# Two layers of graph attention on one core: the second tile's count and the first tile's columns put ahead of two projections in the first part

## Chip, core and metric

The kernel runs on one core of one Trainium2 chip. The metric is the device time of one execution in microseconds (us). The engines work side by side, each through its own queue of instructions in order: PE (TensorE, matrix multiplication; its weight loads are shown apart as PEld), DVE (VectorE), ACT (ScalarE), POOL (GpSimd), and SP (SyncE), which here only issues transfers (DMAs). POOL issues transfers too.

## What is computed

Two layers of graph attention over 3327 nodes with 1024 features, one adjacency matrix for both, each followed by a residual and a layer norm. Cut to what matters:

```python
# layer 0: 8 heads of 128
h = (x @ W).reshape(C, H, D)
alpha_src, alpha_dst = (h * a_src).sum(-1), (h * a_dst).sum(-1)
e = leaky_relu(alpha_src[i] + alpha_dst[j], 0.2);  e = -inf where adj[i, j] == 0
x = layernorm(x + softmax(e) @ h)
# layer 1: one head over 1024 features
h = x @ W1
e = leaky_relu(h @ a1 + (h @ a2).T, 0.2);  e = -9e15 where adj == 0
x = layernorm(x + relu(softmax(e) @ h))
```

The adjacency is symmetric with ones on its diagonal and very sparse: about 0.24% of the pairs are drawn, and each draw counts both ways.

## The kernel before, in words

The nodes are split into 26 tiles of 128 rows (NT = 26). The kernel has a first part that every input goes through, a flag that it computes, and then one of two arms: a dense one, and a sparse one, which this input takes. The sparse arm fetches, for each target tile, the rows of its neighbours with indirect transfers (L803) from a table in memory, h0_d for layer 0 and y_d for layer 1, and adds them with small matmuls.

The first part does two things at once. It projects every tile (x @ W, extended by score columns) and writes the table h0_d; and it turns each tile's 128 rows of the mask into lists of neighbours. Its instructions are put into the queues by hand: the order of the calls in the code is the order on each engine.

The projection of a tile t:

- `load_x(t)`: SP loads the rows; `flip(t)`: 8 transposes on PE in two groups (L176), each followed by copies on ACT and, elsewhere, DVE (in the trace, L179 on ACT).
- `project(t, c)` for c = 0, 1, 2: one third of the columns each, 8 multiplications, which the trace shows as 16 matmul instructions (L479), into one of two PSUM banks with the tag "A".
- `keep(t, c)`: ACT copies the result to SBUF (L496). With c = 2 it also takes out the scores (sd, L491) and two exponentials (L493, L494), and calls `factors(t)`: one ACT operation (r, L295) and four small POOL ones (L296 to L299). After the third keep of a tile SP writes it to h0_d (L499).

The lists of a tile t, class `Edges`:

- `count(t)` calls `words(t)` and then `load_mask(t + 3)`. `words`: POOL clears the diagonal of the mask (`affine_select`, L308); ACT sums each row (junk, L311, with a read of the accumulator) and makes deg_b of it (L313); DVE folds the mask into words in three steps (wd, L318). `load_mask` is a transfer that POOL issues (L468) into one of four mask buffers in turn (the last tile has a fifth), so `load_mask(4)` refills the buffer of tile 0.
- `keys` (two halves) and `columns` (two halves): DVE alone, picking the largest values and removing them (L274, L276, L360, L369 to L375).
- `ends(t)`: one matmul with deg_b (L327), one ACT copy (cnt, L328), seven small POOL operations (L335 to L341). `ends2(t)`: the same manner, matmul L346, ACT L347, POOL L348 to L353.
- `places` (ACT away L384 and L385, DVE L388 to L392), `give` (the xp matmuls, L411 and L401), `take` (ACT L423 to L428), `sources` (DVE L436 to L450).

A generator, `listing()`, strings these steps together. For the first tile its first four steps are the two halves of keys and the two halves of columns; the next, `count(3)`, then the places of tile 0. In the steady loop over tiles 3 to 25, `project` calls `pace()` after every second multiplication, which takes as many steps as keep the lists level with the projections. The start is written out call by call, and there the change lies: projections with `False` don't call `pace()`.

Of the kernel before, what the change touches and what calls it, by code (L numbers as in the profile page):

```python
# [26 lines left out]
def kernel(  # L27
# [129 lines left out]
    class Phase:  # L157
# [7 lines left out]
        def bank(self, tag, shape, name, dt=F32):  # L165
            return self.psum.tile(shape, dt, tag=tag, name=name, bufs=self.banks[tag])
# [286 lines left out]
    with ExitStack() as own, tc.manual_schedule():  # L453
# [10 lines left out]
        def load_mask(t):  # L464
            if t < NT:
                ads[t] = masks[t % 4 if t < NT - 1 else 4]
                for r in pieces(t):
                    nc.gpsimd.dma_start(ads[t][r, :N], adj[at(t, r), :])  # L468
# [6 lines left out]
        def project(t, c, paced=True):  # L475

            acc = accs[t, c] = bank("A", [P, CUTS0[c + 1] - CUTS0[c]], "mm")
            for k in range(KT):
                nc.tensor.matmul(  # L479
                    acc, xT[t][:, k, :], wt[:, k, CUTS0[c] : CUTS0[c + 1]], start=k == 0, stop=k == KT - 1  # L480
                )
                if paced and k % 2 == 1:
                    pace()

        def keep(t, c):
            if t not in hts:
                hts[t] = ph.sbuf("ht", [P, HW0], 4)
            ht, acc, c0 = hts[t], accs.pop((t, c)), CUTS0[c]
            m = min(CUTS0[c + 1], D) - c0
            if c == 2:  # L490
                nc.scalar.activation(sd0[:, t].rearrange("p a h -> p (a h)"), acc[:, m:], AF.Copy)  # L491
                lists[t].factors()
                nc.scalar.activation(ht[:, D : D + H], acc[:, m + H :], AF.Exp)  # L493
                nc.scalar.activation(ht[:, D + H :], acc[:, m + H :], AF.Exp, scale=SLOPE)  # L494
                scored.add(t)
            nc.scalar.activation(ht[:, c0 : c0 + m], acc[:, :m], AF.Copy)  # L496
            kept[t] = kept.get(t, 0) + 1
            if kept[t] == 3:
                nc.sync.dma_start(h0_d[t * P : (t + 1) * P, :], hts.pop(t))  # L499

        def count(t):
            if t < NT:
                lists[t].words(ads.pop(t), junk)
                load_mask(t + 3)

        def listing():

            for t in range(-1, NT):
                old, new = lists[t] if t >= 0 else None, lists[t + 1] if t + 1 < NT else None
                for s in range(4):  # L510
                    if old:
                        old.give(s)
                    if new:
                        (new.keys, new.columns)[s // 2](s % 2)
                    if s == 1 and 2 < t + 3 < NT:
                        lists[t + 3].ends(tri_b)
                    if s == 3 and 2 < t + 3 < NT:
                        lists[t + 3].ends2(all_b)
                    yield
                if old:  # L520
                    old.give(EB)
                    old.take()
                count(t + 4)
                yield
                if old:
                    old.sources()
                    yield
                while new and t + 1 not in scored:
                    yield
                if new:  # L530
                    new.places()
                    yield

        scored, kept = set(), {}
        steps, slots, done = listing(), [0, 0], [0]

        def pace():

            slots[0] += 1
            while done[0] * slots[1] < slots[0] * (7 * (NT + 1)):  # L540
                done[0] += 1
                next(steps, None)
# [90 lines left out]
        count(0)  # L633
        for _ in range(2):
            next(steps)
        project(2, 1, False)
        keep(2, 1)
        project(0, 2, False)
        keep(0, 2)
        lists[0].ends(tri_b)  # L640
        count(1)
        for _ in range(2):
            next(steps)
        project(1, 2, False)
        keep(1, 2)
        lists[0].ends2(all_b)
# [585 lines left out]
```

## Time and profile before

| what | value |
|---|---|
| median of 3 runs | 1955.56 us (1948.99 to 1957.19) |
| the profiled execution | 1903.19 us, of which its span is 1901.5 us |
| mean granted TensorE clock in it | 0.905 |
| first part, from the start to the flag | about 480 us |
| layer 0, sparse arm | about 480 to 1200 us |
| layer 1, sparse arm | about 1200 to 1901 us |

The profile describes one execution, the profiled one, and its stages are told by its clock, from the start of the span. Busy time of each engine by stretch (length; PE, PEld, DVE, ACT and POOL busy with their numbers of instructions; granted TensorE clock; busy share of the 16 DMA engines; GB/s):

```
478.00:530.00 52.00, 17.93 (x301) 14.42 (x301) 22.02 (x54) 4.11 (x15) 31.68 (x30) 0.66 0.90 342
530.00:1200.00 670.00, 401.27 (x7803) 335.39 (x7803) 429.48 (x1038) 166.81 (x485) 437.45 (x416) 0.79 0.98 376
1200.00:1901.00 701.00, 653.41 (x3717) 278.79 (x3717) 295.08 (x856) 144.91 (x253) 440.28 (x441) 0.98 0.93 354
```

Layer 0 has its DMA engines busy nearly all the time, layer 1 has PE busy. In lists of waits and in the timeline, "<-" names what ended an idle time: the engine, what it wrote, and its line. "issue" is time in which an engine waited for nothing that the profile shows.

### The profile page before, as it was taken

Reading aid. Unit: us, or ns where it says so; the run is one execution under the profiler, and the core shown is the slowest. Engines: PE = TensorE matmul, PEld = TensorE weight load, DVE = VectorE, ACT = ScalarE, POOL = GpSimd, SP = SyncE. Lnnn points to the kernel's source line nnn. Section 1 sums busy time; section 2 is a strip of 40 time slices with the busy share of each in tenths; the row PEclk is TensorE's granted clock in tenths of the full one; section 3 lists DMA queues with packets and bytes.
Section 4 is the critical chain, followed back from the end, with each engine's and each line's share of the span. In section 5 each row is a group of like instructions: output and inputs, shape, how many; then the busy total and the mean of one; then the engine's idle time right before and its main releaser. Section 6 shows DMA issues by size and latency. Waiting matters only on the chain.

```text
span 1901.5 us, 38079 instructions
## 1 busy us (share of the span) xinstructions
PE 1518.5 (80%) x14663; PEld 902.4 (47%) x14663; DVE 1146.6 (60%) x3058; ACT 546.6 (29%) x1422; POOL 1030.2 (54%) x1391
## 2 busy tenths in 40 slices
PE   8799999999266555656556565399999999999997
PEld 5465556666255554545545454144444444444443
DVE  6699999986386665666666666244444444444442
ACT  5544455542022222222222222012222212222220
POOL 4322222220576666676676764677766667666650
PEclk9899999999678777787788877699999999999999
DMA  7656455411899999999999997899999999999980
GB/s 184 101 133 131 100 99 99 88 62 39 325 373 404 396 392 394 366 405 392 386 392 389 394 376 273 332 398 410 400 372 382 380 378 369 359 371 373 366 326 33
DMA packets 171068, 567.76 MB, mean 299 GB/s; under 512 B 27690, under 2 KB 34346, under 8 KB 170878
## 3 DMA queue, kind: packets, MB, share of 16 engines
q0 software_dynamic: 131056, 455.68, 67.6%
q1 hardware_dynamic: 39822, 109.56, 15.4%
q8 instruction: 118, 1.93, 0.4%
q14 instruction: 72, 0.59, 0.1%
HBM read 578.85 MB, written 42.97 MB: 327 GB/s over the span
## 4 chain that ended last, share of the span: by engine, by line
PE 52%; DMA 24%; DVE 12%; ACT 6%; issue 4%; POOL 2%; SPq 0%; DVEq 0%; ACTq 0%; POOLq 0%
DMA src<-h_d,idx 20%; PE mm L1025 20%; PE acc L993 12%; PE mm L479 12%; DVE e L870 3%; PE acc L898 3%; ACT junk L311 3%; PE tr L176 2%; POOL src L803 2%; DMA src<-y_d,idx 2%; DVE pr L931 1%; PE acc L882 1%; DMA wt<-in_L_gnn_W_dram 1%; ACT xT L179 1%; PE xp L411 1%
## 5 line engine op out<-in xcount | busy, mean ns | idle before, releaser
L803 POOL DMA_INDIRECT src<-h_d,idx x416 | 441.1, 1060 | 209.1 <-PE acc L898 58.0
L803 POOL DMA_INDIRECT src<-y_d,idx x416 | 415.7, 999 | 221.6 <-PE acc L993 96.3
L898 PE MATMUL acc<-src,e 128*32 128x128 f32 x6656 | 278.5, 337 | 253.6 <-DVE e L870 253.5
L479 PE MATMUL mm<-wt,xT 128*128 128x347 f32 (+1 forms) x1248 | 402.3, 469 | 3.3 <-DMA wt<-in_L_gnn_W_dram 2.9
L1025 PE MATMUL mm<-wt,xT 128*128 128x512 f32 x832 | 383.3, 604 | 0.8 <-DVE o L1028 0.8
L898 PEld LDWEIGHTS acc<-src,e 128*32 128x32 f32 x6656 | 234.8, 137 | 311.3 <-DVE e L870 284.3
L479 PEld LDWEIGHTS mm<-wt,xT 128*128 128x128 f32 x1248 | 228.3, 192 | 106.0 <-issue 4.2
L1025 PEld LDWEIGHTS mm<-wt,xT 128*128 128x128 f32 x832 | 152.2, 190 | 199.5 <-issue 179.1
L993 PE MATMUL acc<-src,es 128*32 128x342 f32 (+1 forms) x2496 | 206.2, 464 | 33.8 <-DVE es L984 31.0
L870 DVE TENSOR_TENSOR e<-oh,way 128x1024 f32<-128x1024 f32 x130 | 158.7, 1221 | 63.2 <-ACT w L868 62.8
L993 PEld LDWEIGHTS acc<-src,es 128*32 128x32 f32 x2496 | 71.6, 111 | 158.6 <-issue 112.9
L868 ACT ACTIVATE w<-way 128x32 f32<-128x32 f32 (+1 forms) x130 | 24.6, 189 | 407.7 <-DVE way L866 395.6
L1028 DVE SCALAR_TENSOR_TENSOR o<-mm,y 128x512 f32<-128x512 f32 x52 | 35.9, 691 | 166.2 <-PE mm L1025 166.2
L1007 ACT ACTIVATE z<-y,ri 128x342 f32<-128x342 f32 (+1 forms) x78 | 39.5, 570 | 313.9 <-DVE ri L1003 313.9
L865 DVE TENSOR_TENSOR way<-src,re 128x32 f32<-128x32 f32 x104 | 20.8, 200 | 175.1 <-DMA src<-h_d,idx 157.6
L179 ACT ACTIVATE xT<-tr 128x512 f32<-128x512 f32 x104 | 59.4, 596 | 151.0 <-PE tr L176 150.9
L981 DVE TENSOR_TENSOR way<-way,src 128x128 f32<-128x128 f32 x104 | 31.1, 299 | 90.0 <-ACT way L951 44.2
L850 ACT ACTIVATE own<-own,es 128x128 f32<-128x128 f32 x208 | 63.6, 388 | 57.4 <-DVE es L847 57.4
L311 ACT ACTIVATE junk<-ad 128x3328 uint8<-128x3328 uint8 x26 | 78.4, 3014 | 2.5 <-POOL ad L308 2.5
L882 PE MATMUL acc<-end,e 128*128 128x128 f32 x416 | 67.7, 328 | 13.3 <-DVE e L870 13.3
L296 POOL CAST mvs<-r 128x8 bf16<-128x8 f32 x26 | 6.0, 232 | 122.8 <-ACT r L295 122.8
L335 POOL TENSOR_TENSOR place_of<-cnt 128x1 f32<-128x1 f32 x26 | 4.9, 190 | 121.0 <-ACT cnt L328 101.5
(188 smaller groups left out, 1959.7 us busy)
## 6 DMA issues: line engine op xcount, KB each, us to landing
h_d<-ht SPq DMA_DIRECT2D x26, 520.0 KB
own<-h_d SPq DMA_DIRECT2D x26, 520.0 KB
y_d<-y SPq DMA_DIRECT2D x26, 514.0 KB
y<-y_d SPq DMA_DIRECT2D x26, 514.0 KB
x<-in_x_dram SPq DMA_DIRECT2D x25, 512.0 KB
y<-in_x_dram SPq DMA_DIRECT2D x25, 512.0 KB
out_dram<-o SPq DMA_DIRECT2D x25, 512.0 KB
ad<-in_adj_dram POOLq DMA_DIRECT2D x25, 415.9 KB
```

The source lines that it names most:

```text
L176: nc.tensor.transpose(tr[:, k, :], src[:, (4 * g + k) * P : (4 * g + k + 1) * P], ident)
L179: nc.scalar.activation(part, tr, AF.Copy)
L311: nc.scalar.activation(junk, ad, AF.Copy, accum_out=self.deg)
L479: nc.tensor.matmul(acc, xT[t][:, k, :], wt[:, k, CUTS0[c] : CUTS0[c + 1]], start=k == 0, stop=k == KT - 1)
L803: nc.gpsimd.indirect_dma_start(out=s[:, g, :w], out_offset=None, in_=table[:, :], in_offset=bass.IndirectOffsetOnAxis(ap=idx[:, t, b * NG ...
L850: nc.scalar.activation(hn, hn, AF.Copy, scale=es[:, n : n + 1])
L870: nc.vector.tensor_tensor(e, oh.unsqueeze(2).to_broadcast([P, ng, H, wide]), wp.unsqueeze(3).to_broadcast([P, ng, H, wide]), OP.mult,)
L882: nc.tensor.matmul(self.acc[h // 4][:, h % 4, :], e[:, 0, h, :], rowsof[:, 0, h, :], start=False, stop=h % 4 == 3,)
L898: nc.tensor.matmul(self.acc[h // 4][g * GT : (g + 1) * GT, h % 4, :], e[:, g, h, :], rowsof[:, g, h, :], start=first and h % 4 == 0, stop= ...
L993: nc.tensor.matmul(self.acc[c][to, :m], es[:, g, :], s[:, g, CUTS[c] : CUTS[c + 1]], start=b == 0, stop=b == EB,)
L1007: nc.scalar.activation(z[:, cut], self.res[:, cut], AF.Copy, scale=ri[:, 1:2])
L1025: nc.tensor.matmul(acc, xT[:, k, :], wt1[:, k, half], start=k == 0, stop=k == KT - 1)
```

## The change

Four lines move up by five calls. In the start of the first part, `count(1)` and the next two steps of the listing, which are the two halves of the columns of tile 0, now come straight after `count(0)` and the two halves of the keys, ahead of `project(2, 1)`, `keep(2, 1)`, `project(0, 2)`, `keep(0, 2)` and `lists[0].ends(tri_b)`. `count(1)` brings along its `load_mask(4)`. No instruction is added or removed.

```diff
         count(0)
         for _ in range(2):
             next(steps)
+        count(1)
+        for _ in range(2):
+            next(steps)
         project(2, 1, False)
         keep(2, 1)
         project(0, 2, False)
         keep(0, 2)
         lists[0].ends(tri_b)
-        count(1)
-        for _ in range(2):
-            next(steps)
         project(1, 2, False)
         keep(1, 2)
         lists[0].ends2(all_b)
```

What follows in the code is unchanged: `lists[1].ends(tri_b)`, `flip(3)`, `load_x(5)`, `flip(4)`, `count(2)`, and then the paced projections.

## Prediction

> **What bounds the kernel now.** I read the page first, for its stages, then the busy time in stretches of 4 us around the place of the edit, then the waits between 54 and 74 us, the timeline there, and last the chain of waits.
>
> ```profile
> span 1901.5 us, 38079 instructions
> PE 1518.5 (80%) x14663; PEld 902.4 (47%) x14663; DVE 1146.6 (60%) x3058; ACT 546.6 (29%) x1422; POOL 1030.2 (54%) x1391
> 0.00:478.00 478.00, 445.89 (x2842) 273.80 (x2842) 400.02 (x1112) 230.75 (x669) 120.79 (x505) 0.99 0.49 104
> ```
>
> The third line gives the first part (0 to 478 us): length, busy us of PE, PEld, DVE, ACT, POOL, granted clock, DMA share, GB/s. PE works 446 of 478 us, so what fills or makes a PE gap here counts. All moved instructions run between 45 and 65 us. The waits of 54 to 74 us show where PE stands still there (who waited, for whom, us in total, times, longest):
>
> ```profile
> PE xp L411 <- DVE place L391: 7.3, 1, 7.3
> PE op L327 <- ACT deg_b L313: 1.9, 1, 1.9
> PE tr L176 <- ACT cnt L328: 0.7, 1, 0.7
> DVE wd L318 <- POOL ad L308: 8.0, 2, 6.6
> ```
>
> The timeline gives their place (start, duration, engine, line, operation, idle before it and its releaser):
>
> ```profile
> 48.89 0.19 ACT L311 ACTIVATION_READ_ACCUMULATOR junk<-ad 128x1 f32 x1
> 49.12 0.21 ACT L313 ACTIVATE deg_b<-cnt 128x1 bf16<-128x1 f32 x1
> 50.34 0.46 ACT L496 ACTIVATE ht<-mm 128x347 f32<-128x347 f32 x1 [1.02 <-PE mm L479]
> ...
> 54.83 4.90 PE L479 MATMUL mm<-wt,xT 128*128 128x346 f32 x16
> ...
> 58.26 2.98 ACT L311 ACTIVATE junk<-ad 128x3328 uint8<-128x3328 uint8 x1 [2.31 <-POOL ad L308]
> ...
> 61.36 0.21 ACT L313 ACTIVATE deg_b<-cnt 128x1 bf16<-128x1 f32 x1
> 61.47 0.17 ACT L491 ACTIVATE sd<-mm 128x16 f32<-128x16 f32 x1
> 61.62 0.16 PE L327 MATMUL op<-deg_b,tri_b 128*128 128x1 bf16 x1 [1.89 <-ACT deg_b L313]
> 62.46 1.09 PE L176 MATMUL tr<-ident,x 128*128 128x128 f32 x8 [0.68 <-ACT cnt L328]
> ```
>
> The count of tile 1 (junk, 58.26) stands behind the seven small POOL operations of `ends(0)`, because its `affine_select` (L308, 57.94) does. It ends with deg_b at 61.57. PE had finished `project(1, 2)` at 54.83 + 4.90 = 59.73; the keep of that result (sd, L491) starts only at 61.47, behind the count on ACT, and PE's next instruction, the matmul of `ends(1)`, waits 1.89 us for deg_b. The chain runs here junk, deg_b, sd, r, the POOL operations of `factors(1)`, `ends2(0)`, `ends(1)`, the `affine_select` of tile 2, then
>
> ```profile
> 65.77 3.08 ACT junk L311 x2
> 68.87 0.04 ACT deg_b L313
> 68.91 0.06 issue
> 68.98 3.06 ACT junk L311 x2
> ```
>
> then the away operation, place (72.91) and PE's first xp matmul at 73.46, which ends the 7.3 us gap.
>
> **What the Trainium skill says.** "PSUM — Partial Sum Buffer", section "Engine vs sequencer instructions": the queues of ScalarE, VectorE and GpSimdE are strict FIFO. So an instruction put ahead delays all behind it if it waits. The trace agrees: sd (L491) has its data at 59.73 and starts when deg_b ahead of it is through, at 61.47. "TensorE: Matmul & The Clock Gate", section "What's actually happening": a pause of one window of about 3.4 us halves PE's clock, and the window runs freely. The trace agrees in kind: after the 7.3 us gap four matmul instructions took 2.67 us, against 1.33 us at 64.78. "DMA: Bandwidth & Descriptors", section "Issuing engines are not separate DMA queues": loads from SP and POOL share 16 engines. Here the engines have room where the moved load goes: their share is 0.00 in 52 to 56 us.
>
> **The change, part by part.** Nothing is added or removed. `count(1)` and columns(0) go ahead of two projections with their keeps and ahead of `ends(0)`.
>
> *PE and SP*: the order of their instructions is unchanged, since count, columns and key steps at this point issue none. SP's write of h0_d(0) and its loads pass nothing.
>
> *DVE*: its order is unchanged too; the projections and keeps moved past issue nothing there. It only stops waiting: the 6.60 us before wd at 58.26. Words of tile 1 (0.59 + 0.67) follow the keys at 51.66 and end near 52.9; columns(0) took 59.48 to 64.4, 4.9 us, and end near 57.9. This gain of 6.5 us has no taker, as its next work, the words of tile 2 (65.77), waits for POOL and its place step for ACT's away. Value 0.
>
> *POOL*: `affine_select` (0.29) and the issue of `load_mask(4)` (0.62) leave 57.94 to 58.79 and come after the issue of mask 3 (ends 45.65). The select needs mask 1, issued at 23.72; the DMA share is 0.81 in 28 to 32 us and 0.01 in 32 to 36, so it landed before 36. The select runs at 45.67. `load_mask(4)` refills the buffer of mask 0 and must wait for ACT's reading of it, through deg_b at 49.33 (the trace shows this very wait once, 2.5 us for deg_b, at the load issued at 69.13). Behind it on POOL is `factors(0)`, due at 55.49: 49.33 + 0.6 = 49.9, cover 5.6 us. Cost 0. The mask itself comes 8 to 9 us earlier, into free engines, and its first user, at 85.25, followed POOL's own work and not a landing. Value 0.
>
> *ACT*: junk(1) and deg_b(1), 58.26 to 61.57 = 3.31 us with the accumulator read, go ahead of keep(2, 1). New times: 49.33 to 52.6. Keep(2, 1) then runs 52.6 to 53.1 instead of 50.34 to 50.80, 2.3 us late. Its PSUM bank is next wanted by `project(1, 2)` at 54.83: cover 1.7 us. Keep(0, 2) starts with PE's end at 55.00, as now. Cost 0, with a thin cover.
>
> *What comes off the path*: deg_b(1) exists at 52.6, long before PE wants it, and ACT is free when `project(1, 2)` ends. sd then starts at 59.73 + 0.05 = 59.78 (the pair of 54.96 and 55.01 in the chain shows the 0.05) and not at 61.47: 1.69 us. The PE wait of 1.89 us goes; the next PE wait, for cnt (L347, 0.75 after sd, its keep lying between), shifts with sd: the flip starts near 60.75 instead of 62.46. POOL was in chain from r (61.67) to the select of tile 2 (65.75) without slack and shifts by the same 1.69; its own select and load no longer lie ahead of it. Then junk(2), junk(3), away, place, xp follow as before: xp at 71.77 instead of 73.46. What is late next is ACT's pair of counts, whose 7.3 us gap stays entire.
>
> *Whether it arrives at the end*: from 73.46 to 475 us I followed the chain: PE matmuls, ACT counts, DVE keys and lists alternate, and no DMA is in it, so there is nothing fixed in time to wait at, and no later order differs. At 480 us a flag is read, then the gathers start; they too shift. Forecast: -1.7 us in the profiled execution, 1901.5 to 1899.8.
>
> *Not shown by this trace*: the phase of the clock window after the 7.3 us gap. Slow matmuls cost (2.61 - 1.27) + (3.50 - 2.53) = 2.3 us by the chain. With the gap 1.7 us earlier the slow stretch can be shorter or longer; bounds, an estimate from these 2.3 us and the page's window: half a window, 1.7 us, either way. I take 0.
>
> The profiled execution took 1903.19 us, with 1.69 us around its span. The median of the runs shown is 1955.56, 52 us more, with the reason in no view; the gain lies in a stage at clock 0.99, so I carry it over as it is: 1955.56 - 1.7 = 1953.9.
>
> **The rivals.**
> *Absorbed, no gain*: 1955.6. For it: in 150 to 400 us DVE is on the chain again and again (92.8 busy of 100 in 300 to 400), and the second part is bound by gathers at a DMA share of 0.98. Against it: the order there is untouched and every queue is shifted alike.
> *The count blocks ACT, slower*: place, junk(1) ahead of keep(2, 1). If the select of tile 1 came no earlier than now (57.94), ACT would stand before keep(2, 1) until junk ends; deg_b at 61.57, keep to 62.0, and `project(1, 2)`, waiting for the bank, would run 62.0 to 66.9, its sd at 67.0 against 61.47: +5.5, so 1961. It decides from junk(1) starting after 49.33 + 1.7 (cover used up) + 1.7 (gain used up) = 52.7. Against it: mask 1 landed some 10 us before the select's new place, and POOL is free at 45.65.
> *More than forecast*: DVE's 6.5 us turn out useful, or the shorter low stretch of PE spares the slow clock after the gap. At most 1.7 + 2.3 + 1.7 = 5.7: 1950. Against: the gap of 7.3 us stays, and DVE waits for POOL anyway.
>
> **How the numbers follow.** Forecast 0.60, absorbed 0.24, blocked 0.09, more 0.07. The runs before spread from 1948.99 to 1957.19, so a median of a few runs can miss by about 4 us: this, more than any cost, makes the range. From 1950 - 4 = 1946 to 1961, opened by a little because the 52 us between profile and runs are unexplained: 1945 to 1962. About 0.5%, 9.8 us, is what a measurement of this kernel can tell from no change; no case reaches it without noise or an unseen effect: faster 0.06, same 0.85, slower 0.09.
>
> **What would show it.** Right: junk(1) starts at 49.3, the load of mask 4 is issued near 49.4, the wait of PE for deg_b is gone, the flip of tile 3 starts near 60.8, the first xp near 71.8, and the first part ends 1.7 us earlier. Wrong: a new PE wait for keep(2, 1) (L496) before 54.83, a POOL wait reaching past 55.5, junk(1) still behind `ends(0)`, or a first part that ends where it does now.

## The result and the profile after

The changed kernel takes 1958.89 us (median of 16 runs, 1950.73 to 1971.35), the kernel before, run beside it, 1958.56 us (16 runs, 1948.99 to 1968.26). The ratio is 1.0011, with a 95% interval of 0.999 to 1.0032: no difference that the measurement can tell. The forecast, 1.7 us less or 0.9991, lies inside the interval, and so does no change at all. The median lies in the stated range of 1945 to 1962 us and 5.0 us above the 1953.9 that was forecast; 3.0 us of these are the base, which was 1955.56 us as the median of three runs and is 1958.56 as that of sixteen, and the other 2.0 are within the scatter of the runs. A range that holds no change as well says little about the mechanism, so what the edit did has to be read from the trace.

The page of the changed kernel, its lines on the span and the engines, and the busy time of the first part (columns as before):

```profile
span 1958.3 us, 38079 instructions
PE 1661.6 (85%) x14663; PEld 936.8 (48%) x14663; DVE 1143.4 (58%) x3058; ACT 546.2 (28%) x1422; POOL 1028.7 (53%) x1391
```

```profile
0.00:478.00 478.00, 447.20 (x2842) 274.35 (x2842) 399.65 (x1111) 230.88 (x669) 121.49 (x505) 0.98 0.49 104
```

The span is 57 us longer than in the profile of before, with the same number of instructions, and the first part is not where it lies: the flag comes at 480.93 us, against 480.16. Before any cause is sought in the edit, the same kernels must be profiled again: the experiments begin with that.

The waits of the changed kernel between 54 and 74 us:

```profile
PE xp L411 <- DVE place L391: 7.3, 1, 7.3
DVE wd L318 <- POOL ad L308: 6.2, 1, 6.2
...
PE tr L176 <- ACT cnt L328: 1.0, 1, 1.0
```

PE's wait of 1.9 us for deg_b is gone, the gap of 7.3 us ahead of the first xp is entire. The timeline of the changed kernel, at the place of the edit:

```profile
50.62 0.21 ACT L313 ACTIVATE deg_b<-cnt 128x1 bf16<-128x1 f32 x1
50.73 2.96 ACT L311 ACTIVATE junk<-ad 128x3328 uint8<-128x3328 uint8 x1
50.89 0.55 POOL L468 DMA_DIRECT2D ad<-in_adj_dram  x1 [3.34 <-ACT deg_b L313]
...
53.82 0.20 ACT L313 ACTIVATE deg_b<-cnt 128x1 bf16<-128x1 f32 x1
53.93 0.44 ACT L496 ACTIVATE ht<-mm 128x347 f32<-128x347 f32 x1
...
56.33 4.90 PE L479 MATMUL mm<-wt,xT 128*128 128x346 f32 x16
...
61.10 0.16 PE L327 MATMUL op<-deg_b,tri_b 128*128 128x1 bf16 x1
61.27 0.18 ACT L491 ACTIVATE sd<-mm 128x16 f32<-128x16 f32 x1 [3.81 <-PE op L327]
...
62.28 1.09 PE L176 MATMUL tr<-ident,x 128*128 128x128 f32 x8 [1.02 <-ACT cnt L328]
```

This execution reached the place of the edit 1.5 us later than the profiled one of before (`project(1, 2)` at 56.33, not 54.83), so absolute times can't be compared. Counted from `project(1, 2)`, sd comes after 4.94 us, against 6.64 before: 1.70 us earlier. Marks used below: A, the start of tile 0's `affine_select` (L308); B, PE's matmul of `ends(0)` (L327), just ahead of that projection; X, PE's first xp matmul.

### The profile page after: what moved, and what is told of

Read it like the earlier page. It is cut to its first block, busy times and chain, and to the rows that moved or that the text cites. A ratio compares the mean times of both kernels' runs of the same rounds, so it can differ in the third digit from the quotient of the medians.

```text
span 1958.3 us, 38079 instructions
## 1 busy us (share of the span) xinstructions
PE 1661.6 (85%) x14663; PEld 936.8 (48%) x14663; DVE 1143.4 (58%) x3058; ACT 546.2 (28%) x1422; POOL 1028.7 (53%) x1391
## 4 chain that ended last, share of the span: by engine, by line
PE 72%; issue 11%; DVE 7%; ACT 5%; DMA 3%; POOL 1%; another core or an unknown queue 1%; SPq 0%; POOLq 0%; ACTq 0%; DVEq 0%
PE mm L1025 19%; PE acc L898 17%; PE acc L993 12%; PE mm L479 12%; PE acc L882 4%; PE acc L890 3%; ACT junk L311 2%; PE tr L176 2%; DMA src<-y_d,idx 1%; DMA wt<-in_L_gnn_W_dram 1%; PE den L907 1%; POOL src L803 1%; DMA src<-h_d,idx 1%; PE xp L411 1%; DVE top L274 1%
## 5 line engine op out<-in xcount | busy, mean ns | idle before, releaser
L898 PE MATMUL acc<-src,e 128*32 128x128 f32 x6656 | 379.3, 304 | 168.3 <-issue 135.3
L993 PE MATMUL acc<-src,es 128*32 128x342 f32 (+1 forms) x2496 | 215.2, 467 | 40.7 <-DVE es L984 24.7
L882 PE MATMUL acc<-end,e 128*128 128x128 f32 x416 | 94.3, 418 | 1.7 <-DVE e L870 1.7
L882 PEld LDWEIGHTS acc<-end,e 128*128 128x128 f32 x416 | 87.7, 321 | 2.3 <-DVE e L870 1.8
L1001 DVE TENSOR_TENSOR ri<-acc,es 128x1 f32<-128x1 f32 x26 | 4.1, 158 | 125.0 <-PE acc L993 110.2
```

The costliest lines, as they stand in the source:

```text
L882: nc.tensor.matmul(self.acc[h // 4][:, h % 4, :], e[:, 0, h, :], rowsof[:, 0, h, :], start=False, stop=h % 4 == 3,)
L898: nc.tensor.matmul(self.acc[h // 4][g * GT : (g + 1) * GT, h % 4, :], e[:, g, h, :], rowsof[:, g, h, :], start=first and h % 4 == 0, stop= ...
L993: nc.tensor.matmul(self.acc[c][to, :m], es[:, g, :], s[:, g, CUTS[c] : CUTS[c + 1]], start=b == 0, stop=b == EB,)
```

## The experiments

Each line is one profiled execution (of a timed kernel, the one of its runs that was profiled); all times in us.

| run | B to sd of tile 1 | B to X | PE's gap before X | B to the flag | span |
|---|---|---|---|---|---|
| before, first profile | 6.67 | 18.66 | 7.34 | 425.36 | 1901.5 |
| before, again | 6.68 | 19.19 | 6.42 | 426.64 | 1901.6 |
| columns alone ahead | 6.68 | 19.15 | 6.21 | 427.07 | 1899.9 |
| changed, first profile | 4.97 | 16.96 | 7.33 | 424.63 | 1958.3 |
| changed, again | 4.97 | 16.95 | 7.33 | 424.30 | 1894.9 |
| count alone ahead | 4.96 | 16.95 | 7.32 | 424.52 | 1895.2 |
| changed, timed | 4.96 | 16.97 | 7.34 | 424.48 | 1957.3 |
| count(2) early too | 4.97 | 13.78 | 4.14 | 420.85 | 1892.9 |
| count(2) ahead of keep(2, 1) | 6.28 | 15.08 | 4.14 | 422.93 | 1895.5 |
| changed, pacing lower | 4.97 | 16.96 | 3.85 | 423.51 | 1897.6 |
| count(2) early, pacing lower | 4.96 | 13.77 | 0.65 | 417.50 | 1892.0 |
| the same, timed | 4.96 | 13.79 | 0.67 | 417.54 | 1962.2 |

**Both kernels again.** No edit.

> The kernel before, unchanged, profiled once more. Two marks: A, the start of tile 0's affine_select (L308), and X, PE's first xp matmul (L411). Theory (the edit's own effect sits between A and X, the rest is scatter of one execution): X - A is 28.6 us again, as in the first profile of before, whatever A itself is, and the span comes out near 1957, not 1901.5, so the 57 us between the first two profiles are not the edit's. Rival (the changed order costs time later): the span is again near 1901.

> The changed kernel, unchanged, profiled once more. Theory: X - A is 26.9 us again, 1.7 less than before. From A to the flag (L699) it needs between 433.5 and 435 us: the first profiles show 435.32 before and 434.60 after, and the slow stretch of PE after the gap moves this by about 1 us either way. Rival (the 1.7 us were luck of one execution's start): X - A lies between 27.5 and 28.6.

Before: X - A was 29.14 where 28.6 was expected, and the span 1901.6 where I had expected 1957. Changed: X - A 26.92 as expected, A to the flag 434.27, span 1894.9. So the 57 us come and go with the same kernel: the changed one has spans of 1894.9 and 1957.3. Between these two, B to the flag is 424.30 and 424.48; the flag to the first gather of y_d takes 714.6 and 751.6, the rest 701.1 and 725.8. The two were run on different chips, and the longer one shows a wait that the other doesn't. PE's largest wait between 530 and 1190 us, first the changed kernel as timed (1957.3), then the changed kernel again (1894.9):

```profile
PE acc L898 <- issue: 137.4, 349, 1.1
```

```profile
PE acc L898 <- DVE e L870: 227.4, 95, 6.2
```

In the longer one PE halts 349 times for nothing that the profile shows. Whether the chip or something else makes it do so was not tried; it is no work of the edit, as the kernel before, timed beside the longer one, took as long (1953.22 to 1972.27 us).

The 0.5 us that the kernel before took longer to X the second time is PE's clock. PE from the matmul of `ends(1)` to the first quarter of `project(2, 2)`, in the second profile of before:

```profile
61.70 0.16 PE L327 MATMUL op<-deg_b,tri_b 128*128 128x1 bf16 x1 [1.89 <-ACT deg_b L313]
62.53 1.09 PE L176 MATMUL tr<-ident,x 128*128 128x128 f32 x8 [0.68 <-ACT cnt L328]
63.88 1.97 PE L176 MATMUL tr<-ident,x 128*128 128x128 f32 x8 [0.25 <-ACT xT L179]
65.64 1.99 PE L479 MATMUL mm<-wt,xT 128*128 128x346 f32 x4
```

The second group of eight transposes took 1.97 us and the four matmuls 1.99, against 1.15 and 1.33 in the first profile. The granted clock, third number from the end of the line for 64 to 66 us, was halved, first the first profile of before, then the second:

```profile
64.00:66.00 2.00, 2.00 (x12) 1.29 (x10) 0.64 (x2) 1.55 (x4) 1.77 (x10) 1.00 0.94 324
64.00:66.00 2.00, 2.00 (x9) 1.98 (x10) 0.60 (x3) 1.02 (x3) 1.77 (x10) 0.50 0.91 322
```

In the second it is 0.50 from 63.57 to 66.98 us, and PE was busy for 1.20 us of the 3.41 us ahead of that. The late copies then held ACT's count of tile 2 back by 0.5 us.

**The two halves of the edit apart.** The edit moves three lines, the count and the two-line loop of the columns. The count alone, shown against the changed kernel, and the columns alone, against the kernel before:

```diff
         count(1)
-        for _ in range(2):
-            next(steps)
...
         lists[0].ends(tri_b)
+        for _ in range(2):
+            next(steps)
```

> Only count(1) goes ahead, the columns of tile 0 stay where they were. Theory (ACT's and POOL's place for the count is the whole effect, DVE's place is worth nothing): X - A is 26.9 us as with the full change; DVE ends the columns about 4.9 us after ends(0), before its words of tile 2. Rival (the columns count too): X - A is over 27.3.

```diff
         count(0)
-        for _ in range(2):
+        for _ in range(4):
             next(steps)
...
         count(1)
-        for _ in range(2):
-            next(steps)
```

> Only the columns of tile 0 go ahead, count(1) stays behind ends(0). Theory: X - A is 28.6 us, nothing gained, PE's wait of 1.9 us for deg_b stays. Rival (freeing DVE is what gains): X - A is below 28.2.

The count alone gives X - A of 26.91, as the full edit. My expectation for DVE missed: the columns began at 53.28, not behind `ends(0)`. The calls between issue nothing on DVE, so moving the columns past them moves nothing; this kernel has the same queues as the changed one, and the run repeats it. The columns alone do change DVE's order (they pass the words of tile 1), and they gain nothing: PE's wait of 1.89 us for deg_b is there, X - A is 28.63, B to X 19.15, with the slow transposes again (1.94), at a granted clock of 0.50 from 61.95 to 65.36 us. Its B to the flag, the longest of all, holds another 1.7 us between the sd operations of tiles 3 and 4, where the granted clock fell to 0.50 once more, from 89.3 to 92.7 us. So the count is what gains. It was moved whole, with its work on ACT, POOL and DVE; that ACT's part is the one that counts was not tried apart, but read from the timeline, where sd stood behind deg_b.

**One more count ahead.** The changed kernel with `count(2)` one place further up, behind `keep(2, 1)`:

```diff
         keep(2, 1)
+        count(2)
         project(0, 2, False)
...
         flip(4)
-        count(2)
```

> The changed kernel with count(2) put between keep(2, 1) and project(0, 2). Marks from here on: B, PE's matmul of ends(0) (L327), and X, the first xp matmul; X - B was 18.7 to 19.2 us with count(1) behind ends(0) and 16.95 with it ahead. Theory (ACT's counts set X, each worth 3.2 us, as long as what they push back is not wanted): keep(0, 2) comes 1.2 us later, still in time for PE's matmul of ends2(0) (cover 0.4 us), one count leaves the gap: X - B is 13.8 us, and from B to the flag 424.4 becomes about 421.3. Rival (POOL's chain of small operations sets X, the counts only fill it): X - B stays over 16.

B to X 13.78, B to the flag 420.85: the theory holds to 0.5 us, and the rival, that POOL's small operations set X, falls. A count on ACT taken out of the gap is worth 3.2 us at X. POOL's chain still sets where the count that remains begins: it starts at 62.13 us, after 0.18 us of waiting for POOL's select.

**The bank as the limit.** The same, but `count(2)` straight behind `count(1)`, ahead of `keep(2, 1)`:

```diff
         count(1)
+        count(2)
...
         flip(4)
-        count(2)
```

> The changed kernel with count(2) straight behind count(1), so ahead of keep(2, 1). Test of the mechanism by which the prediction could have been slower: the PSUM bank that keep(2, 1) frees. Theory: keep(2, 1) ends 1.3 us after B, project(1, 2) waits that long for its bank, its result comes 1.3 us later than in the changed kernel (sd at B + 6.2 instead of B + 4.97), and X - B is 15.0, the saved count (3.2) less the wait (1.3). Rival (the bank has more slack than worked out): no PE wait, X - B is 13.8.

sd at B + 6.28 and X - B 15.08. The new wait is there, in the timeline of this run:

```profile
55.62 0.21 ACT L313 ACTIVATE deg_b<-cnt 128x1 bf16<-128x1 f32 x1
55.73 0.44 ACT L496 ACTIVATE ht<-mm 128x347 f32<-128x347 f32 x1
...
56.23 4.92 PE L479 MATMUL mm<-wt,xT 128*128 128x346 f32 x16 [1.15 <-ACT ht L496]
```

The mechanism of the slower rival exists, and its size is what the cover leaves: with one count ahead, `keep(2, 1)` ended 1.97 us before `project(1, 2)` (52.93 and 54.90 in the second profile of the changed kernel); a second one, 3.2 us, overran that by 1.3 us. The turning point itself, a junk(1) that starts at 52.7, was not tried.

**The pacing.** With `[6, ...]` for `[9, ...]` PE gets all of `project(2, 2)` before its first xp matmul, not a quarter of it; first on the changed kernel, then with `count(2)` early.

```diff
-        done[0], slots[:] = 4, [9, (NT - 3) * 12 + 13]
+        done[0], slots[:] = 4, [6, (NT - 3) * 12 + 10]
```

> The changed kernel with the pacing started three steps lower, so that PE has 12 to 16 matmul instructions of project(2, 2) before its first xp matmul and not 4. Theory (the gap is time in which PE could do later work): X - B stays 16.95, PE's gap before it shrinks from 7.3 to about 4.2 us, and B to the flag falls by 1 to 3 us. Rival (the lists are late, not PE, so work of PE done early is handed back where DVE sets the pace between 150 and 390 us): B to the flag stays within 0.7 us of 424.4.

> Both edits, count(2) early and the pacing lower. Theory: X - B is 13.8, PE's gap is about 1 us, too short for the slow clock after it, so the first matmuls after X run at 1.3 us for four, not 2.7; from B to the flag about 417 to 420 us. Rival: as in the run with count(2) alone, since DVE and ACT set the pace later.

Alone, the pacing gains 0.97 us to the flag (423.51 against 424.48, the mean of the four profiles of the changed order): just under what the theory said and over what the rival allowed. After the gap of 3.85 us left over PE was slow all the same: the granted clock was 0.50 from 73.6 to 80.4 us, and the four matmuls after X took 2.65 us. With both edits B to the flag is 417.50, 3.35 us less than with `count(2)` alone. Here the gap is 0.65 us and the slow stretch is gone: the granted clock is 1.00 from 29 to 471 us. PE in this run's timed copy:

```profile
64.91 4.82 PE L479 MATMUL mm<-wt,xT 128*128 128x346 f32 x16
70.40 0.24 PE L411 MATMUL xp<-mvs,place 32*128 32x42 bf16 x12 [0.67 <-DVE place L391]
70.56 0.18 PE L346 MATMUL op<-more_b,all_b 128*128 128x1 bf16 x1
70.60 0.16 PE L327 MATMUL op<-deg_b,tri_b 128*128 128x1 bf16 x1
70.63 1.41 PE L479 MATMUL mm<-wt,xT 128*128 128x346 f32 x4
```

**Timed against the kernel before**, on one chip: the changed kernel, and the one with both further edits.

> The changed kernel, timed against the kernel before on one chip. Theory: the first part ends 1.9 us earlier from B on (424.5 against 426.4, means of three profiles each), and nothing gives it back, so the ratio is 0.999, within what the measurement tells from 1. Rival (an unseen cost later, as the first comparison's 1.0011 may hint): 1.001 or more.

> The changed kernel with count(2) early and the pacing lower, timed against the kernel before. Theory: from B to the flag 417.5 us against 426.4, 8.9 us less, of about 1900 to 1960: ratio 0.9953 to 0.9955 if the parts after the flag take as long as ever. Rival (the start of the gathers is not what ends last, or scatter of the later parts): 0.998 or more.

Changed: 1959.82 us (14 runs) against 1961.47 (23 runs), ratio 0.9992, interval 0.9968 to 1.0016: the value of the theory, but the interval holds the rival's too. Both edits: 1948.99 us (10 runs), ratio 0.9935, interval 0.9911 to 0.9959. The interval doesn't hold 1, so this one is faster than the kernel before, and the 0.9955 that follows from the 8.9 us of the traces lies inside. The parts after the flag scatter too much to say whether the median's 12.5 us hold more than these 8.9: the profiled execution of this very kernel has a span of 1962.2.

## Why the prediction was right

The second profile of the changed kernel has its mark A at 44.90, next to 44.84 in the profile that the prediction read, so its steps can be checked in absolute times.

- *ACT*: junk(1) was forecast at 49.3, ran at 49.30; keep(2, 1) was to end at 53.1 and ended at 52.93, with `project(1, 2)` at 54.90. No wait.
- *POOL*: the load of mask 4 was forecast near 49.4 and was issued at 49.45, after 3.33 us of waiting for deg_b; `factors(0)` came at 55.57, untouched. Cost 0, as said. The engines were not free, though: the prediction's share of 0.00 is that of 52 to 56 us, while the load was issued in a stretch that had 0.76 before (48 to 52 us), and with it the share was 0.94 from 48 to 56 us. Between 44 and 75 us no wait was for a transfer.
- *DVE*: the columns began at 53.01, and DVE then waited 6.20 us for the words of tile 2. No taker, as said; the run with the columns alone shows the same from the other side.
- *The path*: sd at 59.84 (forecast 59.78), the flip at 60.84 (60.75), X at 71.82 (71.77). The forecast of -1.7 at X is met within 0.05 us.
- *To the end of the first part*: B to the flag is 426.4 us on the mean of the three profiles with `count(1)` behind `ends(0)` and 424.5 on the mean of the four with it ahead, 1.9 less. The three scatter by 1.7 us, the four by 0.3, so that pairs give 0.7 to 2.8. That the means differ by so nearly 1.7 is in part luck. Up to X the gain is 2.04 us, 1.70 of them the edit's and 0.34 from a slow clock ahead of the gap, which two of the three have. From X to the sd of tile 2 0.69 are lost, from there to that of tile 4 0.62 gained, where the columns alone have their second low clock, and 0.09 lost after that. The rival of a gain absorbed on the way is ruled out for the first part: from the sd of tile 4 to that of tile 25 it takes 359.6 to 359.8 us in the three profiles of the old place of `count(1)` and the four of the new, and from there to the flag 15.9 in all, so this stretch gives nothing back.
- *The clock after the gap*, taken as 0 within 1.7 either way: from X to the sd of tile 2 it took 6.72, 7.40 and 5.91 before and 7.29 to 7.47 changed, 0.7 more on the mean. It follows how long the granted clock stayed at 0.50 past X: 5.2, 6.6 and 3.6 us before, 6.4 to 6.7 changed, and each us of it costs half a us. The term is real and inside its bounds. What the step left out is the slow clock before the gap, which costs 0.5 us at X: two of three profiles of the old order have it, and none of the four of the new, where PE's wait of 1.89 us is gone. That this wait sets it off is likely, but not shown apart.
- *To the median*: the total can't show 1.7 us, as the prediction said. That the gain reaches the end of the kernel is consistent with the second ratio, 0.9992, but not shown. From the flag to the end the three short profiles of the old order took 1419.9 to 1421.3 us and the two of the new (changed again, count alone) 1415.7 and 1415.5, those with the further edits 1417.4 to 1419.2. These profiles show nothing given back. Most of what their spans differ by lies there, 4 to 6 us; it was not forecast, and no run here tells its cause.

## What to carry to other kernels

In a start that is written out by hand, ask of each long instruction what stands behind it in its queue and when that is wanted: 3.3 us of ACT work cost 1.7 us in one place and nothing in another, and a second such piece beside it there cost 1.3 us. Where one engine's gap is left entire by an edit, the edit has only shifted it; the larger gain came from taking work out of the gap (3.2 us for a count) and from giving the waiting engine later work, and the second paid 0.97 us while a gap of 3.85 us was left and 3.35 us when only 0.65 was. A gain of 0.1% is read in the trace from a mark next to the edit, not from the total, and the same kernel should be profiled twice before a difference is explained.

## What was not expected of the hardware

PE's granted clock fell to 0.50 after waits of 1.89 and 0.68 us around a single 0.16 us matmul in two of three profiles, and didn't in the third: the same queue, 1.97 or 1.94 against 1.15 us for eight transposes. The prediction had only a pause of about 3.4 us slow PE; here PE had been busy for 1.20 and 1.33 us of the 3.41 us ahead of the fall. Every stretch at 0.50 that begins between 20 and 480 us lasts 3.41 us or a whole multiple of it in all twelve traces, and it begins at another place in the queue from one profile to the next. Gaps of 3.85 us and of 6.21 to 7.34 us were each followed by four matmuls at 2.65 to 2.68 us, the two of 4.14 us by 2.68 in one run and 1.81 in the other, where the clock fell only 0.9 us after these matmuls had begun; a gap of 0.65 us was followed by four at 1.41. And the same kernel took 1895 us on one chip and 1957 on another, with equal first parts (424.30 and 424.48 us from B to the flag).
